# A two-layer graph network in fp32: other order of VectorE's work, statistics shared with ScalarE, other order of loads in the head

## The chip, the cores and the metric

The kernel runs on one core of one Trainium2 chip. The metric is the device time in microseconds of one execution, as the median of three runs. The profiled execution is one more run, with its own time and span.

## The reference

64 samples of 256 tokens with 512 channels go through two layers. Each begins with a layer norm and a relu and ends with a residual sum.

```python
# layer 0
h = maximum(layernorm(x), 0)
q, k, v = h @ Wq.T, h @ Wk.T, h @ Wv.T            # per sample, 256 x 512
rel = adj.T * (q @ k.T)                           # 256 x 256
rel = rel / norm(rel, axis=2)                     # each row by its length
x = x + rel @ v
# layer 1
h = maximum(layernorm(x), 0)
y = adj @ h
x = x + y @ weight + bias
```

All is fp32; adj holds only 0 and 1.

## The kernel before

The kernel takes two samples at a time, a pair: 512 tokens, in four chunks of 128 rows; 32 pairs in all. Chunk c is sample c // 2, token half c % 2. Wq and Wk are multiplied into one matrix M in the head (`before_pairs`), so that the scores are h M h'. Every large product is done by Strassen's scheme in Winograd's form: seven products of half size, numbered 1 to 7, and sums of operands (`left_factors`, `right_operands`) on VectorE; some are split so once more (`two_levels`: g1 to g4 are the products of the second level). Product n goes into a PSUM bank; `take` moves the result out, by a ScalarE copy the first time and by a VectorE addition the next times, always in the order in which the program has them. Products 1, 6, 7 and 4 go into bank_a one after the other, so each of them waits until VectorE or ScalarE has read the one before.

The order of work on TensorE, VectorE and ScalarE is written out by hand: inside `tc.manual_schedule` each of the three carries out its instructions in the order of the program. A list of steps is given to `run_steps`, and a dictionary `side` tells which other work is issued behind which step ("slot" in what follows). DMAs are issued by SP, by ScalarE and by GpSimd.

Software pipelining runs over the pairs: `first_pairs`, then 28 times `steady(i)`, then `last_pairs`. A call of `steady(i)` does, in this order:

- `attend_and_v(i)` (L676): the scores of pair i times v, added to x (take L672), mixed with the rest of v of pair i+1 (L516, L537). When it is done, x of pair i is the input of layer 1. Its token half 0 is complete behind slot 4, its token half 1 behind slot 6.
- `ln1(i)` (L691): statistics of layer 1 by `norm` (L322): for each chunk a BN_STATS (L333) and a BN_AGGR (L334) on VectorE; then the root (L337, L338), its inverse (L341, L342), and the relu on ScalarE (L345), split into an upper and a lower part (L710, L714).
- `scores(i+1)` (L545): seven products (L314), takes L560 (ScalarE) and L562 (VectorE), masks by adj, squares, scaling by the inverse length; then `place`, 16 DMAs on SP that move 32x32 blocks, and `turns` (L592), four VectorE transposes inside those blocks. Together they transpose the scores.
- `g_and_v(i+2)`: h M and h Wv'.
- `gather_steps(i)` (L729): y = adj h (L742), four PSUM tiles, each copied to yt by ScalarE (L746); and `y_steps`, the four sums over yt for the product that follows: `y_steps[0]` (L176), `y_steps[1]` (L177, the operand of product 5; it adds the two channel halves of one token half), `y_steps[2]` (L178, the operand of product 6) and `y_steps[3]` (L179).
- `mix_and_v(i)` (L927): y times `weight` (L302), added to x (take L776), with the second level (L528, L537), whose eight sums over 128x128 blocks `second_of_y` gives (L758); then GpSimd's DMA of the pair.

`norm_by_scalar` (L351) is another form of the statistics, for layer 0: the totals by a ScalarE Copy with an accumulator (L361), the squares by a Square with an accumulator (L367).

The head loads adj, Wq, Wk and the first pair, computes M by one Winograd product (`early=True`: products 1, 2, 5, 6, 3, 7, 4), transposes Wv and looks into adj: `look` (L842) takes the lowest 12 bits of all its elements, and a flag `low_any` tells whether any is set. Every engine reads the flag (L906) and branches to one of two programs, `pairs(True)` or `pairs(False)`.

```python
    y_products, y_steps = gather_steps(i, exact)
    run_steps(y_products, {0: v_steps[1:2], 2: y_steps[0:1], 3: turns})
    y_second = second_of_y(i)
    ...
    run(y_steps[1:2])
    mixed = mix_and_v(i, g, v, {
        0: y_steps[2:4] + totals[0:2], 1: y_second[0:4] + totals[2:4],
```

Of the kernel before, what the change touches and what calls it, by code (L numbers as in the profile page):

```python
# [19 lines left out]
def kernel(  # L20
# [39 lines left out]
    P = 128  # L60
# [21 lines left out]
    X, H, HL, G, V, R, H2, Y, HL2, Y2, second_h = ({} for _ in range(11))  # L82
# [5 lines left out]
    def load(i, queue=nc.sync):  # L88
        X[i] = ring[i % len(ring)]
        queue.dma_start(out=X[i], in_=xs[i])  # L90
# [7 lines left out]
    bias_bc = const.tile([P, D], F32, name="bias_bc")  # L98
    nc.scalar.dma_start(out=adj_sb, in_=adj.rearrange("(c p) n -> p c n", p=P))
    for e in range(DC):  # L100
        nc.sync.dma_start(out=wq_sb[:, e], in_=wq[e * P : (e + 1) * P, :])
        nc.scalar.dma_start(out=wk_sb[:, e], in_=wk[e * P : (e + 1) * P, :])
    load(0)
    ones = const.tile([P, 1], F32, name="ones")
# [5 lines left out]

    def load_wv():
        nc.scalar.dma_start(out=wv_sb, in_=wv.rearrange("(c p) d -> p c d", p=P))
# [209 lines left out]
    def norm(src):  # L322

        st = small.tile([P, TC, 6], F32, tag="st", name="st")
        mv = small.tile([P, TC, 2], F32, tag="mv", name="mv")
        rs = small.tile([P, TC], F32, tag="rs", name="rs")
        nb = small.tile([P, TC], F32, tag="nb", name="nb")  # L330

        def chunk(c):
            nc.vector.bn_stats(st[:, c, :], src[:, c, :])  # L333
            nc.vector.bn_aggr(mv[:, c, :], st[:, c, :])  # L334

        def root():
            nc.vector.tensor_scalar(rs, mv[:, :, 1], 0.0, EPS, op0=ALU.max, op1=ALU.add)  # L337
            nc.scalar.activation(rs, rs, AF.Sqrt)  # L338

        def end():  # L340
            nc.vector.reciprocal(rs, rs)  # L341
            nc.vector.scalar_tensor_tensor(nb, mv[:, :, 0], -1.0, rs, op0=ALU.mult, op1=ALU.mult)  # L342

        def relu(dst, c):
            nc.scalar.activation(  # L345
                dst, src[:, c, :], AF.Relu, bias=nb[:, c : c + 1], scale=rs[:, c : c + 1]
            )

        return [(lambda c=c: chunk(c)) for c in range(TC)], root, end, relu
# [40 lines left out]
    def ln0(i):  # L390

        if i == 0:
            H[i] = blocks.rearrange("p c d e -> p c (d e)")
        else:
            H[i] = work.tile([P, TC, D], F32, tag="hy", name=f"h_{i}")
        h = H[i]
        chunks, root, end, relu = norm(flat(X[i]))
        return chunks, root, end, [(lambda c=c: relu(h[:, c, :], c)) for c in range(TC)]
# [292 lines left out]
    def ln1(i, exact):  # L691
# [3 lines left out]
        chunks, root, end, relu = norm(xt)  # L695
# [62 lines left out]
    def second_of_y(i, pool_tag="h2"):  # L758

        room = work.tile([P, 2, 3, P], F32, tag=pool_tag, name=f"ys2_{i}")  # L760
        factors, steps = {}, []
        for k in (2, 3):
            factors[k], more = left_factors(
                lambda b, d, f=Y[i][k]: f[:, d, ts(b, P)], [room[:, k - 2, n] for n in range(3)]
            )
            steps.append(more)
        Y2[i] = factors
        return steps[0][:2] + steps[1][:2] + steps[0][2:] + steps[1][2:]
# [54 lines left out]
    def before_pairs():  # L823
# [18 lines left out]
        def look():  # L842
            nc.vector.tensor_single_scalar(
                low, adj_sb.rearrange("p c n -> p (c n)").bitcast(I32), 0xFFF, op=ALU.bitwise_and
            )
            nc.vector.tensor_reduce(low_max, low, axis=mybir.AxisListType.X, op=ALU.max)
            pf = ps_m.tile([P, 512], F32, tag="pm", name="pf")
            nc.tensor.matmul(pf[0:1, 0:1], low_max, ones, start=True, stop=True)
            nc.vector.tensor_copy(low_any, pf[0:1, 0:1])
# [20 lines left out]
        def take(t, k, bank, first):  # L870
# [7 lines left out]
        look()  # L878
        transpose_adj()
        run([right_steps[1], left_steps[1]])  # L880
        winograd(product_weights_moving(m_left, m_factors), take, {
            0: [load_wv, left_steps[2], right_steps[2]],
            1: [left_steps[3], left_steps[0]],
            2: [right_steps[0]] + stats[0:1] + [lambda: load(1, nc.scalar)],
            3: stats[1:4] + [root, lambda: load(2, nc.scalar)],
            4: [end] + relus + [right_steps[3]],
            5: m_steps[0:3] + [transpose_wv],
# [49 lines left out]
    def first_pairs(exact):  # L937
# [50 lines left out]
        if exact:  # L988
            nc.vector.tensor_copy(adjt_r, adjt_sb)
        g, v = g_and_v(2, by_slot(layer_1(parts), {  # L990
            1: h_second + [inverse], 2: turned3[0:4], 3: scales + [place],
# [12 lines left out]
            2: y_second[4:8] + [mean] + row_squares[0:2], 3: v_steps[1:2] + row_squares[2:4],  # L1004
            4: turns + rel_steps[0:2] + norm0[0:2], 5: rel_steps[2:4] + v_steps[2:3],
# [3 lines left out]
    def steady(i, exact, relu0, v_last, mixed, v):  # L1009
# [6 lines left out]
        stats, root, end, relus, uppers, lowers = ln1(i, exact)  # L1016
        halves = [stats[b * NC + t] for t in range(NC) for b in range(NB)]
        attend_and_v(i, mixed, v, {
            0: relus0[0:2] + v_last, 1: relus0[2:4] + gs[0:1], 2: gs[1:2],
            3: gs[2:3], 4: gs[3:4] + halves[0:1], 5: halves[1:2],  # L1020
        })
        place_blocks(i + 3)
        if i + 4 < NP:
# [4 lines left out]
            0: halves[2:3], 1: halves[3:4] + h_second[0:1], 2: [root] + h_second[1:4],  # L1028
# [13 lines left out]
        run_steps(y_products, {0: v_steps[1:2], 2: y_steps[0:1], 3: turns})  # L1042
# [5 lines left out]
        run(y_steps[1:2])  # L1048
# [8 lines left out]
    def last_pairs(exact, relu0, v_last, mixed, v):  # L1057
# [62 lines left out]
            0: y_second[0:4] + [root], 1: y_second[4:8] + [end] + relus[0:2] + uppers[0:2],  # L1120
# [10 lines left out]
        ], {0: y_steps[2:4], 1: y_second})  # L1131
# [36 lines left out]
```

## Time and profile before

| | |
|---|---|
| median of three runs | 1705.73 us (1705.2 to 1706.16) |
| profiled execution | 1703.48 us, span 1701.4 us |
| granted TensorE clock | 0.999 |
| TensorE matmul, share of the span | 99% |
| VectorE | 87% |
| ScalarE | 48% |
| GpSimd | 13% |
| one steady pair | 51.7 us |
| bytes moved by DMA | 122.56 MB, 72 GB/s |

The clock is full throughout. A matmul's bar in the profile is longer than the distance to the next one, because matmuls overlap, so the share of 99% does not tell what is lost between them; the starts do. In the timeline a row can stand for several instructions of one form (x4): it then gives the start of the first and the time until the end of the last. PEld is the loading of a matmul's stationary operand, and an instruction name with q (PEq, SPq) is the engine's sequencer.

### The profile page before, as it was taken

How to read it: one execution, taken by the hardware profiler on the slowest of the kernel's cores; microseconds unless marked ns; L12 is line 12 of the kernel's file. 1: busy time of each engine (PE TensorE's matmuls, PEld its weight loads, DVE VectorE, ACT ScalarE, POOL GpSimd, SP SyncE). 2: the span in 40 equal slices, each digit the busy share in tenths (PEclk: the TensorE clock that was granted, in tenths of full speed). 3: DMA queues.
4: the chain of work that ended last, by engine and by line, in shares of the span. 5: the costliest groups of instructions: out<-in, count | busy, mean ns of one | idle time of the engine just before them, and what ended most of it. 6: DMA issues, size and time to landing. Idle time of an engine off the chain costs nothing.

```text
span 1701.4 us, 28459 instructions
## 1 busy us (share of the span) xinstructions
PE 1684.2 (99%) x10274; PEld 1530.6 (90%) x10274; DVE 1472.9 (87%) x3312; ACT 811.3 (48%) x1835; POOL 226.7 (13%) x191
## 2 busy tenths in 40 slices
PE   9999999999999999999999999999999999999997
PEld 7979999999899999999999999999999999999986
DVE  7788889888898888898888988888988889888677
ACT  4455444545445554445544455454455544453331
POOL 1211100111101111001111001110011110011111
PEclk9999999999999999999999999999999999999999
DMA  7414332234332233332343322443323433223101
GB/s 247 63 26 87 84 78 57 55 77 87 79 62 68 53 87 85 77 60 63 65 87 80 83 50 50 87 87 77 60 67 60 87 83 80 55 47 62 38 25 53
DMA packets 425734, 122.56 MB, mean 72 GB/s; under 512 B 398064, under 2 KB 398832, under 8 KB 425584
## 3 DMA queue, kind: packets, MB, share of 16 engines
q1 hardware_dynamic: 412992, 80.28, 25.6%
q0 software_dynamic: 8432, 32.51, 5.2%
q10 hardware_dynamic: 4160, 7.87, 1.3%
q8 instruction: 83, 1.36, 0.3%
q14 instruction: 67, 0.55, 0.1%
HBM read 38.27 MB, written 33.55 MB: 42 GB/s over the span
## 4 chain that ended last, share of the span: by engine, by line
PE 91%; DVE 4%; SPq 2%; DMA 1%; ACT 1%; issue 1%; DVEq 0%; ACTq 0%
PE bank_a L302 24%; PE bank_a L290 12%; PE bank_a L314 7%; PE bank_c L302 6%; PE bank_e L528 6%; PE bank_a L665 6%; PE py L742 6%; PE bank_d L528 5%; PE bank_c L314 3%; PE bank_c L290 3%; PE bank_c L665 3%; PE bank_e L481 3%; SPq L589 2%; PE bank_d L481 2%; PE bank_b L314 2%; PE bank_b L665 1%
## 5 line engine op out<-in xcount | busy, mean ns | idle before, releaser
L726 POOL TENSOR_TENSOR x_ring<-x_ring,bias_bc 128x512 f32<-128x512 f32 x128 | 187.2, 1483 | 667.3 <-DVE rel L562 406.2
L302 PE MATMUL bank_a<-wv_t,ht 128*128 128x256 f32 x768 | 181.7, 379 | 0.0
L290 PE MATMUL bank_a<-ht,m_t 128*128 128x256 f32 x768 | 181.4, 379 | 0.0
L290 PEld LDWEIGHTS bank_a<-ht,m_t 128*128 128x128 f32 x768 | 145.9, 190 | 19.8
L302 PEld LDWEIGHTS bank_a<-wv_t,ht 128*128 128x128 f32 x768 | 143.5, 190 | 18.3
L714 DVE TENSOR_TENSOR h<-h2c,h 128x512 fp32r<-128x512 f32 x128 | 85.4, 689 | 80.0 <-ACT h L710 80.0
L516 ACT COPY v<-bank_a 128x512 f32<-128x512 f32 x96 | 55.1, 574 | 206.5 <-PE bank_a L302 206.5
L367 ACT ACTIVATE blocks<-x_ring,sm 128x512 f32<-128x512 f32 x112 | 80.8, 722 | 125.3 <-DVE sm L364 123.5
L742 PE MATMUL py<-adjt_r,h 128*128 128x256 f32 x1024 | 127.1, 281 | 0.5 <-DVE h L714 0.4
L345 ACT ACTIVATE h2c<-x_ring,nb,rs 128x512 f32<-128x512 f32 x128 | 97.3, 809 | 58.0 <-DVE nb L342 51.9
L302 PE MATMUL bank_a<-w_t,ys 128*128 128x256 f32 x512 | 121.4, 380 | 2.2 <-DVE x_ring L776 2.2
L742 PEld LDWEIGHTS py<-adjt_r,h 128*128 128x128 f32 x1024 | 120.9, 189 | 1.0 <-DVE h L714 0.9
L797 POOL DMA_DIRECT2D out_dram<-x_ring x31 | 24.0, 773 | 723.3 <-issue 522.9
L380 ACT ACTIVATE h<-x_ring,nb,rs 128x512 f32<-128x512 f32 x112 | 82.0, 802 | 66.0 <-PE bank_e L528 66.0
L302 PEld LDWEIGHTS bank_a<-w_t,ys 128*128 128x128 f32 x512 | 96.7, 190 | 16.4 <-DVE x_ring L776 3.0
L746 ACT COPY yt<-py 128x512 f32<-128x512 f32 x128 | 74.9, 588 | 70.4 <-PE py L742 47.3
L776 DVE TENSOR_TENSOR x_ring<-bank_a,x_ring 128x512 f32<-128x512 f32 x128 | 87.9, 687 | 23.2 <-PE bank_a L302 23.2
L314 PE MATMUL bank_a<-ht,gt 128*128 128x128 f32 x744 | 101.2, 279 | 0.0
L333 DVE BATCH_NORM_STATS2 st<-x_ring 128x6 f32<-128x512 f32 x144 | 97.6, 678 | 0.4
L560 ACT COPY rel<-bank_a 128x256 f32<-128x256 f32 x96 | 35.7, 372 | 129.6 <-PE bank_a L314 111.1
L314 PEld LDWEIGHTS bank_a<-ht,gt 128*128 128x128 f32 x744 | 90.4, 192 | 2.8
L453 DVE STREAM_TRANSPOSE ht<-blocks 128x256 f32<-128x256 f32 x248 | 87.7, 407 | 0.7 <-DMA blocks<-h 0.7
(223 smaller groups left out, 4012.5 us busy)
## 6 DMA issues: line engine op xcount, KB each, us to landing
blocks<-h SPq DMA_DIRECT2D x496, 64.0 KB, 2.3
out_dram<-x_ring POOLq DMA_DIRECT2D x31, 1024.0 KB, 4.8
x_ring<-in_x_dram SPq DMA_DIRECT2D x28, 1024.0 KB, 5.6
placed<-rel SPq DMA_DIRECT2D x496, 32.0 KB, 2.0
x_ring<-in_x_dram ACTq DMA_DIRECT2D x4, 1024.0 KB, 5.3
wq_sb<-in_L_gnn_Wq_dram SPq DMA_DIRECT2D x4, 256.0 KB, 4.8
wk_sb<-in_L_gnn_Wk_dram ACTq DMA_DIRECT2D x4, 256.0 KB, 6.0
wv_sb<-in_L_gnn_Wv_dram ACTq DMA_DIRECT2D x1, 1024.0 KB, 5.6
```

Source lines behind the costliest of these rows:

```text
L290: nc.tensor.matmul(bank[:, e * HT_ : (e + 1) * HT_], right[n][:, d, ts(e, P)], left[n][:, d, :], start=(start and e == 0 and d == 0), stop ...
L302: nc.tensor.matmul(bank[:, b * HD : (b + 1) * HD], left[n][:, d, ts(b, P)], right[n][:, d, :], start=(start and b == 0 and d == 0), stop=( ...
L314: nc.tensor.matmul(bank[:, ts(b, P)], right[n][:, d, ts(b, P)], left[n][:, d, ts(b, P)], start=(start and b == 0 and d == 0), stop=(d == H ...
L333: nc.vector.bn_stats(st[:, c, :], src[:, c, :])
L345: nc.scalar.activation(dst, src[:, c, :], AF.Relu, bias=nb[:, c : c + 1], scale=rs[:, c : c + 1])
L453: nc.vector.transpose(ht[:, d, half].rearrange("p (b n) -> p b n", b=NB), by_half[:, :, half, d])
L528: nc.tensor.matmul(out, left[k][n], right[k][n], start=start, stop=True, skip_group_check=True)
L665: nc.tensor.matmul(bank[:, ts(b, HD)], left[n][:, b], right[n][:, b], start=(start and b == 0), stop=True, skip_group_check=True,)
L714: nc.vector.tensor_sub(dst[:, 1, c, :], whole_h[c], dst[:, 0, c, :].bitcast(F32))
L726: (lambda c=c: add(xt[:, c, :], xt[:, c, :], bias_bc, ALU.add)) for c in range(TC)
L742: nc.tensor.matmul(pm[:, d, :], left[:, b * NC + m, ts(d0 + d, P)], right, start=(n == 0), stop=(n == len(terms) - 1),)
L776: nc.vector.tensor_add(xt[block], bank.rearrange("p (b e) -> p b e", b=NB), xt[block])
```

## The change

Five things are changed.

- In `steady`, `turns` leave slot 3 of the gather and go behind `y_steps[1]`, so that VectorE does the sum first and then the four transposes.
- `norm` can be given a scratch tile, `junk`. Then chunks 0 and 2 (token half 0 of both samples) get their mean and their squares by ScalarE (`totals`, `squares`), with two small VectorE operations: the sign change of the means and the division of the squares (`variances`). Chunks 1 and 3 stay with BN_STATS. It is used for layer 0 of the first pair (with room in h) and for layer 1 in `steady` (with room behind the tile of `second_of_y`, which gets 10 blocks instead of 6). In `steady` the totals are issued behind slot 4 of `attend_and_v`, the squares behind slot 5, the variances and chunk 1 behind slot 0 of the scores, chunk 3 behind slot 1.
- Head: Wq and Wk are loaded by four blocks of 256 rows x 256 columns instead of four blocks of 128 rows; adj is loaded after them; Wv's load is issued at once instead of behind product 1. The look at adj and its transposes move from the start to slots 4 and 5 of the product; reading the flag's sum from PSUM becomes `find`.
- `first_pairs`: the scaling of the scores and `place` go one slot earlier, ahead of four block transposes.
- `last_pairs`: the eight sums of the second level are split over slots 1 and 2, four each, in the last two products.

```diff
+    for k in range(2):
+        for j in range(2):
+            block = (slice(None), slice(j * HC, (j + 1) * HC), slice(k * HD, (k + 1) * HD))
+            nc.sync.dma_start(out=wq_sb[block], in_=wq.rearrange("(c p) d -> p c d", p=P)[block])
+            nc.scalar.dma_start(out=wk_sb[block], in_=wk.rearrange("(c p) d -> p c d", p=P)[block])
     nc.scalar.dma_start(out=adj_sb, in_=adj.rearrange("(c p) n -> p c n", p=P))
-    for e in range(DC):
-        nc.sync.dma_start(out=wq_sb[:, e], in_=wq[e * P : (e + 1) * P, :])
-        nc.scalar.dma_start(out=wk_sb[:, e], in_=wk[e * P : (e + 1) * P, :])
     load(0)
+    nc.scalar.dma_start(out=wv_sb, in_=wv.rearrange("(c p) d -> p c d", p=P))
...
-    def norm(src):
+    def norm(src, junk=None):
...
+        def totals():
+            for c in (0, 2):
+                nc.scalar.activation(
+                    junk, src[:, c, :], AF.Copy, scale=1.0 / D, accum_out=mv[:, c, 0:1]
+                )
+
+        def squares():
+            minus = small.tile([P, TC], F32, tag="minus", name="minus")
+            nc.vector.tensor_single_scalar(minus[:, 0::2], mv[:, 0::2, 0], -1.0, op=ALU.mult)
+            for c in (0, 2):
+                nc.scalar.activation(
+                    junk, src[:, c, :], AF.Square, bias=minus[:, c : c + 1],
+                    accum_out=mv[:, c, 1:2],
+                )
+
+        def variances():
+            nc.vector.tensor_scalar(
+                mv[:, 0::2, 1], mv[:, 0::2, 1], 0.0, 1.0 / D, op0=ALU.max, op1=ALU.mult
+            )
...
+        chunks = [(lambda c=c: chunk(c)) for c in range(TC)]
+        if junk is not None:
+            chunks = [totals, squares, variances] + chunks[1::2]
...
-        room = work.tile([P, 2, 3, P], F32, tag=pool_tag, name=f"ys2_{i}")
+        rooms = 6 if pool_tag == "hs2" else 10
+        room = work.tile([P, rooms * P], F32, tag=pool_tag, name=f"ys2_{i}")
+        junk[i] = room[:, 6 * P :]
...
-        look()
-        transpose_adj()
         run([right_steps[1], left_steps[1]])
         winograd(product_weights_moving(m_left, m_factors), take, {
-            0: [load_wv, left_steps[2], right_steps[2]],
+            0: [left_steps[2], right_steps[2]],
             1: [left_steps[3], left_steps[0]],
             2: [right_steps[0]] + stats[0:1] + [lambda: load(1, nc.scalar)],
-            3: stats[1:4] + [root, lambda: load(2, nc.scalar)],
-            4: [end] + relus + [right_steps[3]],
-            5: m_steps[0:3] + [transpose_wv],
+            3: stats[3:4] + stats[1:2] + [right_steps[3], lambda: load(2, nc.scalar)],
+            4: stats[4:5] + [look, stats[2], root, end] + relus,
+            5: m_steps[0:3] + [transpose_wv, find, transpose_adj],
             6: m_steps[3:4],
         }, early=True)
...
-            1: h_second + [inverse], 2: turned3[0:4], 3: scales + [place],
+            1: h_second + [inverse], 2: scales + [place] + turned3[0:4],
...
-        halves = [stats[b * NC + t] for t in range(NC) for b in range(NB)]
         attend_and_v(i, mixed, v, {
             0: relus0[0:2] + v_last, 1: relus0[2:4] + gs[0:1], 2: gs[1:2],
-            3: gs[2:3], 4: gs[3:4] + halves[0:1], 5: halves[1:2],
+            3: gs[2:3], 4: stats[0:1] + gs[3:4], 5: stats[1:2],
         })
...
-            0: halves[2:3], 1: halves[3:4] + h_second[0:1], 2: [root] + h_second[1:4],
+            0: stats[2:4], 1: stats[4:5] + h_second[0:1], 2: [root] + h_second[1:4],
...
-        run_steps(y_products, {0: v_steps[1:2], 2: y_steps[0:1], 3: turns})
+        run_steps(y_products, {0: v_steps[1:2], 2: y_steps[0:1]})
...
-        run(y_steps[1:2])
+        run(y_steps[1:2] + turns)
...
-            0: y_second[0:4] + [root], 1: y_second[4:8] + [end] + relus[0:2] + uppers[0:2],
+            0: [root], 1: y_second[0:4] + [end] + relus[0:2] + uppers[0:2], 2: y_second[4:8],
...
-        ], {0: y_steps[2:4], 1: y_second})
+        ], {0: y_steps[2:4], 1: y_second[0:4], 2: y_second[4:8]})
```

## The prediction

> **What bounds the kernel now.** I read the page first: the busy shares, then the chain that ended last.
>
> ```profile
> PE 1684.2 (99%) x10274; PEld 1530.6 (90%) x10274; DVE 1472.9 (87%) x3312; ACT 811.3 (48%) x1835; POOL 226.7 (13%) x191
> ...
> PE 91%; DVE 4%; SPq 2%; DMA 1%; ACT 1%; issue 1%; DVEq 0%; ACTq 0%
> ```
>
> TensorE holds the chain almost throughout, and no edit takes a matmul away, so only its stalls can move. They are found in the timeline as distances between the starts of neighbouring matmuls above 0.216 us (256 columns) or 0.112 (128). That makes some 34.5 us: 6 in the first 30 us, 18.4 in the 28 steady pairs of 51.7 us each, 7.6 after 1580 us. Two places of a steady pair matter.
>
> Place A, the product of y with the last weight, in pair 4: VectorE's timeline, then TensorE's (start, duration, engine, line, operation, idle before).
>
> ```profile
> 319.77 0.68 DVE L176 TENSOR_TENSOR ys<-yt 128x512 f32<-128x512 f32 x1
> 320.42 1.42 DVE L592 STREAM_TRANSPOSE turned<-placed 128x256 f32<-128x256 f32 x4
> 321.77 0.65 DVE L177 TENSOR_TENSOR yt<-yt 128x512 f32<-128x512 f32 x1
> 322.69 0.69 DVE L776 TENSOR_TENSOR x_ring<-bank_a,x_ring 128x512 f32<-128x512 f32 x1 [0.27 <-PE bank_a L302]
> 323.30 0.68 DVE L178 TENSOR_TENSOR ys<-yt 128x512 f32<-128x512 f32 x1
> ```
> ```profile
> 320.69 1.89 PE L302 MATMUL bank_a<-w_sb,yt 128*128 128x256 f32 x8
> 322.57 1.97 PE L302 MATMUL bank_c<-w_sb,yt 128*128 128x256 f32 x8
> 324.37 1.89 PE L302 MATMUL bank_a<-w_t,ys 128*128 128x256 f32 x8
> ```
>
> The four transposes fill the time until ScalarE's fourth copy of y ends (321.47). Then comes the sum (L177), for which product five (322.57) waits; then L776, which empties bank_a, and L178, which product six (324.37) needs. Six loses nothing. Over 28 pairs five loses 6.5 us, 0.23 a pair; in six of them the transposes' DMA lands late and it is 0.5 to 0.8.
>
> Place B, the scores, VectorE and then product four:
>
> ```profile
> 345.47 0.69 DVE L672 TENSOR_TENSOR x_ring<-bank_a,x_ring 128x512 f32<-128x512 f32 x1 [0.37 <-PE bank_a L665]
> 346.08 0.41 DVE L537 TENSOR_TENSOR v<-bank_e,v 128x256 f32<-128x256 f32 x1
> 346.41 0.68 DVE L537 TENSOR_TENSOR v<-bank_d,v 128x512 f32<-128x512 f32 x1
> 347.01 0.68 DVE L333 BATCH_NORM_STATS2 st<-x_ring 128x6 f32<-128x512 f32 x1
> 347.72 0.18 DVE L334 BATCH_NORM_AGGREGATE mv<-st 128x2 f32<-128x6 f32 x1
> 347.82 0.66 DVE L672 TENSOR_TENSOR x_ring<-bank_a,x_ring 128x512 f32<-128x512 f32 x1
> 348.40 0.41 DVE L537 TENSOR_TENSOR v<-bank_e,v 128x256 f32<-128x256 f32 x1
> 348.73 0.68 DVE L333 BATCH_NORM_STATS2 st<-x_ring 128x6 f32<-128x512 f32 x1
> ```
> ```profile
> 353.06 1.16 PE L314 MATMUL bank_a<-ht,gt 128*128 128x128 f32 x8
> ```
>
> VectorE is idle before 345.47, so it is caught up there; from 347.01 it runs without a gap to L562 (352.59), which empties bank_a for product four. That product already loses 0.17 us a pair.
>
> In the head, TensorE's timeline and what is said of the flag that picks the program's branch:
>
> ```profile
> 20.64 1.89 PE L302 MATMUL bank_a<-wk_t,wq_sb 128*128 128x256 f32 x8
> 22.36 1.91 PE L431 MATMUL pt<-ident,blocks 128*128 128x128 f32 x16
> ```
> ```profile
> L849 DVE CAST low_any<-pf x1: 145/145/145, 6.1 to 6.1; 1x1 int32<-1x1 f32 x1
> ...
> L906 PEldq TENSOR_LOAD <-low_any x1: 486/486/486, 20.3 to 20.3; - x1
> ```
>
> The flag is ready at 6.2 us, so TensorE's sequencer can read it at 20.3, ahead of the matmuls, and the branch costs nothing.
>
> **What the Trainium skill says.** Perfetto Trace Analysis, "Sequencer Loop": an instruction goes into its engine's queue and waits there for its semaphores, while a control instruction is executed by the sequencer. The trace agrees: in place A L776 starts only after what stands before it, and the flag's load runs 2 us ahead. DMA: Bandwidth & Descriptors, "Issuing engines are not separate DMA queues": transfers from SP and ACT share the same 16 engines and interleave. Here the 16 engines are full from 4 to 12 us (384 and 370 GB/s). VectorE: DVE Perf Modes, "Two Vector instructions with no wait between them": an accumulating operation is two instructions. On ScalarE the trace shows the pair, 0.63 and 0.19 us (L361).
>
> **The change, part by part.** The sum is against the profiled execution (1703.48 us, span 1701.4); the median of the runs is 2.25 higher.
>
> *Sum ahead of the transposes (28 steady pairs).* No work is added. The sum cannot use the 0.7 us that the transposes filled, since it adds both channel halves and needs the fourth copy: it starts at 321.50 instead of 321.77. Behind it, in VectorE's order: sum 0.60 (start to start), transposes 1.34, L776 0.61, L178 0.68: ready at 324.73, TensorE at 324.78. Product six without any loss would be at 320.69 + 16 x 0.216 = 324.15. So it loses 0.63 plus about 0.08 for the first interval: 0.70. The copy's end moves by under 0.1 between pairs, so this holds in each. Product five's wait goes, late DMAs are covered (the transposes start 1.7 later), but six waits for the queue instead. Three hundredths more for the second-level sums behind it: 0.73 - 0.23 = +0.50, x 28 = **+14.0**. Bounds +11 to +17.
>
> *Statistics (28 pairs).* Off VectorE: two chunks, 0.68 + 0.18 each; on: two small operations of 0.17. ScalarE gets two Copy (0.81 start to start) and two Square (0.85). In place B: ScalarE's copy of v (L516) starts at 344.61, the totals run 345.10 to 346.63. VectorE's sign change follows L537 at 347.01, the squares run 347.20 to 348.87. VectorE now does L672 when TensorE is done with it (347.4, not 347.82) and L537 at 348.0, is free at 348.33, and then stands before the variances until 348.90. The next chunk starts at 348.98 instead of 348.73, and behind it stands everything up to L562. Product four is 0.25 later: **+7.0**. ScalarE's L560 comes 0.07 late, which its bank's next product covers by 0.2. The chain through ScalarE has no example in the trace: if it is hidden, product four's own 0.17 goes (-4.8); if L560 and one more wake-up count too, +0.45 (+12.6). I take +0.25, since every duration in it has a row.
>
> *Head.* Wq and Wk land as before, in 1 KB pieces; product one needs one block of each and not two. Product five needs the fourth Wq block (8.4 landed now, 8.6 then), the sum (0.69): 9.5 instead of 11.98, -2.5. But Wv's load no longer waits behind ScalarE's first copy (issue 9.57); it is issued while the engines are full and shares them with x. Some 0.75 MB more lie ahead of x's end: 12.05 becomes about 14.3 at 377 GB/s. The totals of x stand on ScalarE before product six's copy: 14.3 + 1.6 + 0.6 = 16.5, and product seven, which reuses that bank, starts there instead of 17.16. The flag's matmul and four transposes of the adjacency move from idle time into the stream: 0.55. Product four is then at about 20.6, as before: the gain is spent. Now the flag: on VectorE, from 16.5, come an addition 0.6, a chunk 0.8, the look 1.2, the statistics' end 1.1, an addition 0.7, three m steps 2.15, two copies 1.2, the cast 0.15: 24.4. Reading it and branching took TensorE 0.75 at 20.3; L431 comes at 25.2 and not 22.36: +2.8. Of that 0.7 returns, since product five of the next stage no longer waits (26.46). **+2.1**, bounds -2 (x lands as before, the flag hidden) to +3.5.
>
> *First pairs.* The scales and 16 score DMAs go ahead of four transposes, 1.6 earlier; the turns that need them (123.3) waited for no DMA, so nothing is won. ScalarE's copy of v stands behind the scales: **+0.2** (0 to +0.6).
>
> *Tail.* In the last product but one L776 of product six stood behind eight 128x128 steps (it ran at 1670.01); with four of them it runs at 1669.1: -0.95. In the last one likewise, 1688.46 to 1687.41: -1.05. **-2.0** (-1.5 to -3).
>
> Sum: 14.0 + 7.0 + 2.1 + 0.2 - 2.0 = **+21.3**: 1724.8 for the profiled execution, 1727.0 for the median.
>
> **Rivals.**
> 1. *VectorE's relief carries through* (faster). VectorE is 87% busy and loses about 1.3 us a pair; if it reaches both places ahead of time, the waits go: -6.5 - 4.8, with head, first pairs and tail -11.0: 1694.7. It decides only if the sum can start by 320.8 and the squares end by 348.3. Against it: VectorE was idle or waiting just before both places, so being ahead buys nothing there.
> 2. *ScalarE's chain is hidden.* Place A as worked out, B at 0 to -4.8: about 1717.
> 3. *Place B is worse*, the +0.45 a pair: 1732.6.
> 4. *Place A is smaller*, product six hidden for a reason not seen and B as worked out: 1713.
>
> **Numbers.** Chances: mine 0.53, rival 1 0.11, 2 0.14, 3 0.13, 4 0.09. The predicted time is the likeliest case's, 1727. The range, 1714 to 1737, takes in rivals 2 and 3, the bounds of A and the head, and leaves out rival 1. A measurement of this kernel tells about 0.2% from no change (1702.3 to 1709.1): faster 0.11, the same 0.03 (the edges of 1 and 4), slower 0.86.
>
> **What would show it.** Right: the transposes of the scores start after the sum, and product six in bank_a begins 0.6 to 0.8 us late in every steady pair, while five starts on time; L562 of product seven ends 0.25 later after TensorE's L665; the pair takes 52.5 us instead of 51.73; the flag's load on TensorE begins at about 24. Wrong: a steady pair of 51.5 us or less, or product six on time. Then the time is 1700 or below, and my order of VectorE's queue or its start at the fourth copy is at fault.

## The result, and the profile after

The kernel is slower: 1727.42 us (median of four runs, 1727.29 to 1727.8) beside 1705.95 for the kernel before (four runs, 1705.2 to 1707.43); ratio 1.0125, 95% interval 1.0108 to 1.0143. The profiled execution took 1727.55 us, span 1725.5. The lines of the new kernel are shifted against those shown so far: L333 is now L335, L592 is L617, L672 is L697, L776 is L804, L562 is L587, L537 is L562 and L431 is L456.

The page of the new kernel, busy shares and then the chain:

```profile
PE 1691.6 (98%) x10274; PEld 1531.6 (89%) x10274; DVE 1430.1 (83%) x3254; ACT 895.4 (52%) x2067; POOL 218.5 (13%) x191
...
PE 66%; DVE 15%; SPq 7%; ACT 5%; issue 3%; DMA 3%; DVEq 0%; ACTq 0%
```

VectorE lost 43 us of work and ScalarE gained 84, yet VectorE's share of the chain went from 4% to 15%: it has less to do and is waited for more. Where this happens is read from the starts of TensorE's matmuls. The execution is cut at the first matmul of a gather:

| stretch (profiled executions, us) | before | after | difference | predicted |
|---|---|---|---|---|
| start to the first gather | 107.24 | 110.95 | +3.71 | head +2.1 |
| to the first steady gather | 54.06 | 54.91 | +0.85 | first pairs +0.2 |
| 28 steady pairs | 1451.27 | 1471.18 | +19.91 | +21.0 |
| to the gather of the last pair but one | 39.70 | 39.72 | +0.02 | 0 |
| to the gather of the last pair | 24.29 | 24.89 | +0.60 | -0.95 |
| to the end of the span | 24.84 | 23.84 | -1.00 | -1.05 |

**Place A.** VectorE's timeline of the new kernel, then TensorE's; columns as before (start, duration, engine, line, operation, idle before and who ended it):

```profile
326.49 0.69 DVE L176 TENSOR_TENSOR ys<-yt 128x512 f32<-128x512 f32 x1
328.34 0.69 DVE L177 TENSOR_TENSOR yt<-yt 128x512 f32<-128x512 f32 x1 [1.17 <-ACT yt L771]
328.95 1.42 DVE L617 STREAM_TRANSPOSE turned<-placed 128x256 f32<-128x256 f32 x4
330.29 0.65 DVE L804 TENSOR_TENSOR x_ring<-bank_a,x_ring 128x512 f32<-128x512 f32 x1
330.86 0.67 DVE L178 TENSOR_TENSOR ys<-yt 128x512 f32<-128x512 f32 x1
```
```profile
327.52 1.89 PE L302 MATMUL bank_a<-w_sb,yt 128*128 128x256 f32 x8
329.25 1.89 PE L302 MATMUL bank_c<-w_sb,yt 128*128 128x256 f32 x8
331.59 1.99 PE L302 MATMUL bank_a<-w_t,ys 128*128 128x256 f32 x8 [0.45 <-DVE ys L178]
```

VectorE now idles 1.17 us before the sum, where the transposes used to be, and does them when product six (331.59) is next in line. Product five starts 1.73 after product one, that is on time; product six 2.34 after five. Over the 28 pairs six loses 0.725 us a pair (0.62 before it and 0.105 behind its first matmul), five nothing (0.233 before). With place B, below, a steady pair takes 52.54 us on the mean, 51.83 before.

**Place B.** VectorE, then product four of the scores on TensorE:

```profile
354.33 0.16 DVE L346 TENSOR_SCALAR minus<-mv 128x2 f32<-128x2 f32 x1
354.71 0.69 DVE L697 TENSOR_TENSOR x_ring<-bank_a,x_ring 128x512 f32<-128x512 f32 x1 [0.22 <-PE bank_a L690]
355.32 0.41 DVE L562 TENSOR_TENSOR v<-bank_e,v 128x256 f32<-128x256 f32 x1
356.22 0.17 DVE L354 TENSOR_SCALAR mv<-mv 128x2 f32<-128x2 f32 x1 [0.49 <-ACT ys L348]
356.30 0.69 DVE L335 BATCH_NORM_STATS2 st<-x_ring 128x6 f32<-128x512 f32 x1
```
```profile
360.63 1.16 PE L314 MATMUL bank_a<-ht,gt 128*128 128x128 f32 x8 [0.15 <-DVE rel L587]
```

VectorE, freed of two chunks here (0.68 and 0.18 us each), stands 0.49 us before the variances (L354) until ScalarE's second square (L348) is done. Product four loses 0.414 us a pair instead of 0.172.

**Head.** TensorE's timeline of the new kernel:

```profile
20.57 2.00 PE L302 MATMUL bank_a<-wk_t,wq_sb 128*128 128x256 f32 x8
24.83 3.46 PE L456 MATMUL pt<-ident,blocks 128*128 128x128 f32 x16 [2.27 <-ACT adjt_sb L888]
28.08 2.08 PE L290 MATMUL bank_a<-ht,m_sb 128*128 128x256 f32 x8
```

The transposes of h (L456) start 2.47 us later than before (22.36), because TensorE stands at the branch until the flag has been read, at 24.0:

```profile
L934 PEldq TENSOR_LOAD <-low_any x1: 488/488/488, 24.0 to 24.0; - x1
```

In addition the sixteen transposes take 3.46 us and not 1.91: one in 0.2 us instead of 0.109. What that is, the last section shows.

### The profile page after: what moved, and what is told of

Read it like the earlier page. It is cut to its first block, busy times and chain, and to the rows that moved or that the text cites. A ratio compares the mean times of both kernels' runs of the same rounds, so it can differ in the third digit from the quotient of the medians.

```text
span 1725.5 us, 28632 instructions
## 1 busy us (share of the span) xinstructions
PE 1691.6 (98%) x10274; PEld 1531.6 (89%) x10274; DVE 1430.1 (83%) x3254; ACT 895.4 (52%) x2067; POOL 218.5 (13%) x191
## 3 DMA queue, kind: packets, MB, share of 16 engines
q1 hardware_dynamic: 413504, 80.28, 25.2%
q8 instruction: 83, 1.36, 0.3%
## 4 chain that ended last, share of the span: by engine, by line
PE 66%; DVE 15%; SPq 7%; ACT 5%; issue 3%; DMA 3%; DVEq 0%; ACTq 0%
PE bank_a L302 19%; PE bank_a L290 12%; SPq L468 7%; PE py L767 7%; PE bank_e L553 4%; PE bank_c L302 4%; PE bank_c L290 3%; PE bank_e L506 3%; PE bank_d L553 3%; PE bank_a L690 3%; ACT h L405 3%; PE bank_a L314 3%; DVE st L335 2%; PE bank_d L506 2%; DVE turned L617 2%
## 5 line engine op out<-in xcount | busy, mean ns | idle before, releaser
L751 POOL TENSOR_TENSOR x_ring<-x_ring,bias_bc 128x512 f32<-128x512 f32 x128 | 180.5, 1430 | 681.6 <-ACT h2c L367 651.5
L739 DVE TENSOR_TENSOR h<-h2c,h 128x512 fp32r<-128x512 f32 x128 | 85.5, 691 | 80.8 <-ACT h L735 80.8
L367 ACT ACTIVATE h2c<-x_ring,nb,rs 128x512 f32<-128x512 f32 x128 | 97.3, 809 | 59.8 <-DVE nb L364 50.1
L697 DVE TENSOR_TENSOR x_ring<-bank_a,x_ring 128x512 f32<-128x512 f32 x116 | 79.7, 687 | 39.5 <-PE bank_a L690 39.5
L804 DVE TENSOR_TENSOR x_ring<-bank_a,x_ring 128x512 f32<-128x512 f32 x128 | 86.9, 679 | 8.4 <-PE bank_a L302 4.4
L492 ACT COPY g<-bank_a 128x512 f32<-128x512 f32 x96 | 56.0, 583 | 56.3 <-PE bank_a L290 56.3
```

Source lines behind the costliest of these rows:

```text
L367: nc.scalar.activation(dst, src[:, c, :], AF.Relu, bias=nb[:, c : c + 1], scale=rs[:, c : c + 1])
L751: (lambda c=c: add(xt[:, c, :], xt[:, c, :], bias_bc, ALU.add)) for c in range(TC)
L804: nc.vector.tensor_add(xt[block], bank.rearrange("p (b e) -> p b e", b=NB), xt[block])
```

## The experiments

Each is an edit of the changed kernel, unless said otherwise. The runs of the kernel before that stood beside them had medians of 1705.39 to 1706.45. Losses per pair are means over the 28 steady pairs of one profiled execution, taken from the starts of the matmuls.

**1. The transposes back ahead of the sum.**

```diff
-        run_steps(y_products, {0: v_steps[1:2], 2: y_steps[0:1]})
+        run_steps(y_products, {0: v_steps[1:2], 2: y_steps[0:1], 3: turns})
...
-        run(y_steps[1:2] + turns)
+        run(y_steps[1:2])
```

> The changed kernel with the four block transposes back in slot 3 of the gather, ahead of the sum; all else as changed. Queue theory (the transposes' 1.34 us now stand between the sum and the sum for product six): product six loses under 0.1 us a pair instead of 0.73, product five gets back its 0.23; 0.49 x 28 = 13.8 us less, 1713.6. Rival (the late operand comes from ScalarE's statistics and not from the order on VectorE): product six stays late, 1726 to 1728. Rival (both together): about 1720.

Measured: 1715.53 us (1713.68 to 1716.75), ratio to before 1.0054 (1.0037 to 1.0071). Product six loses nothing that can be seen; product five loses 0.35 and not 0.23, since in seven of the pairs the transposes' DMA was so late that five waited 0.6 to 1.1 us. The queue's order is the cause of place A: of its price of 13.8 us, 10.6 came back in the 28 pairs of the profiled execution (11.9 between the medians). The later DMAs, 0.12 us a pair more than before the change, are the rest.

**2. Layer 1's statistics back on VectorE.**

```diff
-        stats, root, end, relus, uppers, lowers = ln1(i, exact, junk.pop(i - 1))
+        stats, root, end, relus, uppers, lowers = ln1(i, exact)
+        halves = [stats[b * NC + t] for t in range(NC) for b in range(NB)]
...
-            3: gs[2:3], 4: stats[0:1] + gs[3:4], 5: stats[1:2],
+            3: gs[2:3], 4: gs[3:4] + halves[0:1], 5: halves[1:2],
...
-            0: stats[2:4], 1: stats[4:5] + h_second[0:1], 2: [root] + h_second[1:4],
+            0: halves[2:3], 1: halves[3:4] + h_second[0:1], 2: [root] + h_second[1:4],
```

> The changed kernel with layer 1's statistics of the steady pairs on VectorE alone, as before the change. Theory (VectorE stands before the variances until ScalarE's squares end): product four of the scores loses 0.17 us a pair instead of 0.41; 0.24 x 28 = 6.7 us less, 1720.7. Rival (that loss comes from somewhere else in the change): no difference, 1726.5 to 1728. Rival (VectorE's relief is worth something elsewhere in the pair): slower than 1728.

Measured: 1721.33 us (1720.68 to 1721.45), ratio 1.0092 (1.0075 to 1.0109). Product four loses 0.173 a pair again, and product six of place A still its 0.73, so that wait does not come from the statistics. The shared statistics cost 6 us; the work that they take off VectorE is worth nothing in this order.

**3. The variances behind chunk 3.** The same work, in another place.

```diff
-            0: stats[2:4], 1: stats[4:5] + h_second[0:1], 2: [root] + h_second[1:4],
+            0: stats[3:4], 1: stats[4:5] + [stats[2]] + h_second[0:1], 2: [root] + h_second[1:4],
```

> The changed kernel with the variances issued behind chunk 3 instead of ahead of chunk 1; no work added or taken away. Theory (the stand before the variances is the whole cost of place B): VectorE reaches the addition that empties bank_a in time, product four loses under 0.1 us a pair instead of 0.41; 9 to 11.5 us less, 1716 to 1718.5. Rival (ScalarE's own chain is late, its four more operations delay its copies of the scores): product four stays at 0.3 to 0.4, 1726 to 1728.

Measured: 1724.33 us (1723.77 to 1726.22), ratio 1.0111 (1.0094 to 1.0128): neither of the two. Product four's loss is gone (0.007 a pair), as the theory said. But product seven of h M, which reuses bank_a, now waits for ScalarE's copy of product six (L492) and loses 0.35. Following that back along the timelines: ScalarE's copy stands behind its scales and squares, the squares need the masked scores, and the two mask multiplications on VectorE (L590) took 1.6 us each, where the changed kernel's first one took 0.68. VectorE's timeline of this run, then GpSimd's:

```profile
359.92 3.23 DVE L590 TENSOR_TENSOR rel<-rel,adjt_sb 128x512 f32<-128x512 f32 x2
```
```profile
359.66 2.94 POOL L751 TENSOR_TENSOR x_ring<-x_ring,bias_bc 128x512 f32<-128x512 f32 x2 [14.74 <-ACT h2c L367]
```

The earlier relus (ScalarE's L367) free GpSimd's addition of the bias (L751) 0.26 us ahead of the first mask; in the trace the additions end at 360.92 and 362.60, and each mask ends 0.56 us after one of them, as if it had only then had its turn. The Trainium skill, SBUF — State Buffer, "Who interferes with whom", has this: a VectorE instruction with two inputs in SBUF contends with a GpSimd instruction that reads SBUF, and whoever comes first holds the shared port to its end. Three more runs try it.

**4. The same, with the additions in another order.**

```diff
+        bias = add_bias(i)
...
-            4: lowers[2:3] + sums[0:1] + add_bias(i),
+            4: lowers[2:3] + sums[0:1] + bias[2:4] + bias[0:2],
```

> The kernel with the variances behind chunk 3, and GpSimd's four additions of the bias in the steady pairs in the order of chunks 2, 3, 0, 1, so that they start some 9 us later, after the masks. Theory (in the run before, the additions, started earlier by the earlier relus, held VectorE's mask multiplications, 1.6 us each instead of 0.68, and through the squares ScalarE's copy for the product of h M): the masks take 0.68, that product doesn't wait, place B loses under 0.1 us a pair; 0.4 x 28 = 11 us less than the changed kernel, 1716. Rival 1 (ScalarE's relus are in the way themselves): as the run before, 1724. Rival 2 (the additions now hold VectorE's subtractions and sums in the products of h M and h Wv): 0.2 to 0.6 us a pair come back there, 1722 to 1733.

Measured: 1726.39 us (1726.24 to 1727.44), ratio 1.0118 (1.0101 to 1.0135). This tells nothing of the theories: GpSimd is not among the engines whose order is written by hand, its first addition started at 359.76 as in the run before (359.66), and product seven lost the same 0.35. It is a repetition of experiment 3, on another chip, and lies 2 us above it. In the 28 pairs of the two profiled executions the difference is 1.7 us, and 1.6 of that is in the gathers, whose matmuls ran 1.5% slower; why was not followed.

**5. The additions left out.** The kernel of experiment 3 without the bias in the 28 steady pairs; that part of the sum isn't computed.

```diff
-            4: lowers[2:3] + sums[0:1] + add_bias(i),
+            4: lowers[2:3] + sums[0:1],
```

> The kernel with the variances behind chunk 3, without GpSimd's additions of the bias in the 28 steady pairs (that part of the sum is left out); nothing else is moved, so relus and inverse stay as early as in that kernel. Theory (the additions hold VectorE's masks): both masks take 0.68 us, the product of h M waits under 0.05 us a pair instead of 0.35; 1714 to 1716. Rival (the early relus on ScalarE were in the way, and moving them back was the cure): the product of h M still waits 0.3 or more, 1723 to 1726.

Measured: 1714.92 us (1714.4 to 1716.35), ratio 1.0054 (1.0037 to 1.0071). VectorE's timeline:

```profile
357.25 0.68 DVE L590 TENSOR_TENSOR rel<-rel,adjt_sb 128x512 f32<-128x512 f32 x1
358.20 0.69 DVE L590 TENSOR_TENSOR rel<-rel,adjt_sb 128x512 f32<-128x512 f32 x1 [0.27 <-ACT rel L585]
```

Without an addition beside them both masks take 0.68 and 0.69, and neither product waits any more. GpSimd's additions were the cause, not the early relus.

**6. The additions kept, the relus later.** The kernel of experiment 3, with the root's inverse and the relus one slot later.

```diff
-            3: [end] + relus[0:1], 4: relus[1:2],
+            4: [end] + relus[0:2],
```

> The kernel with the variances behind chunk 3, and the inverse of the root (two small operations) and both relus one slot later in the scores, behind the addition that empties bank_a; no work added. Theory (GpSimd's additions, freed by the relus, hold the masks): the first addition starts at least 0.6 us later against the scores, the first mask takes 0.68 and is done before it, the second waits at most once; the product of h M waits under 0.1 us and the scores' product four under 0.1; place B 0.4 us a pair less than in the changed kernel, 11 us, 1716. Rival (ScalarE itself is too full there, and the later relus push its copies): the product of h M waits 0.35 or more, 1724 to 1728.

Measured: 1714.55 us (1714.09 to 1715.73), ratio 1.0051 (1.0034 to 1.0068). VectorE's timeline, then GpSimd's:

```profile
358.85 0.68 DVE L590 TENSOR_TENSOR rel<-rel,adjt_sb 128x512 f32<-128x512 f32 x1
360.16 1.06 DVE L590 TENSOR_TENSOR rel<-rel,adjt_sb 128x512 f32<-128x512 f32 x1 [0.63 <-ACT rel L585]
```
```profile
359.26 3.10 POOL L751 TENSOR_TENSOR x_ring<-x_ring,bias_bc 128x512 f32<-128x512 f32 x2 [15.40 <-ACT h2c L367]
```

The first addition now begins 0.41 us after the first mask's start and not 0.26 before it; that mask takes 0.68, the second 1.06. Products four and seven lose under 0.01 a pair. The 28 pairs take 1460.54 us, beside 1460.48 in the run without additions: this order costs nothing more than leaving the additions out.

**7. The transposes still later**, in the product of y.

```diff
-        run(y_steps[1:2] + turns)
+        run(y_steps[1:2])
...
-            3: rel_steps[0:2] + row_squares[2:4], 4: root0 + rel_steps[2:4] + end0,
+            3: turns + rel_steps[0:2] + row_squares[2:4], 4: root0 + rel_steps[2:4] + end0,
```

> The changed kernel with the transposes moved further back, to slot 3 of the mix ahead of the sums over them, so that neither the sum for product five nor that for product six has them ahead of it. Queue theory: neither product waits, 0.73 x 28 = 20.3 us less, 1707. Rival (the transposes only carry the wait to the next place, the addition that empties bank_a for product four of the mix or the first product of the scores times v): 0.3 to 0.6 us a pair come back there, 1715 to 1724.

Measured: 1732.68 us (1730.69 to 1734.6), ratio 1.0161 (1.0144 to 1.0178): the rival's mechanism, and worse than it said. VectorE, then TensorE:

```profile
334.43 1.41 DVE L617 STREAM_TRANSPOSE turned<-placed 128x256 f32<-128x256 f32 x4
335.87 0.42 DVE L176 TENSOR_TENSOR rel<-turned 128x256 f32<-128x256 f32 x1
336.33 0.42 DVE L177 TENSOR_TENSOR turned<-turned 128x256 f32<-128x256 f32 x1
336.68 0.68 DVE L804 TENSOR_TENSOR x_ring<-bank_a,x_ring 128x512 f32<-128x512 f32 x1
```
```profile
337.41 1.99 PE L302 MATMUL bank_a<-w_t,yt 128*128 128x256 f32 x8 [0.65 <-DVE x_ring L804]
```

Five and six wait for nothing, but product four of this stage waits until L804, behind the transposes, has emptied bank_a: 0.92 us a pair where six lost 0.73. From the first L804 (327.73) to that one VectorE runs without a gap, so of the 1.34 us of the transposes 0.92 come out as a wait for the next bank.

**8. Two transposes ahead of the sum, two behind.**

```diff
-        run_steps(y_products, {0: v_steps[1:2], 2: y_steps[0:1]})
+        run_steps(y_products, {0: v_steps[1:2], 2: y_steps[0:1], 3: turns[0:2]})
...
-        run(y_steps[1:2] + turns)
+        run(y_steps[1:2] + turns[2:4])
```

> The changed kernel with two of the four transposes in slot 3 of the gather ahead of the sum, and two behind it. Queue theory: two (0.67 us) fit into VectorE's idle time before the fourth copy of y, the other two mostly into its idle time before product one ends (0.49), so product five starts on time but for late DMAs and product six loses under 0.1; 0.6 to 0.7 us a pair less than the changed kernel, 1708 to 1711. Rival (any transposes behind the sum cost product six their whole time): product six loses 0.3 to 0.4, 1717 to 1719.

Measured: 1709.4 us (19 runs, 1707.93 to 1711.24), ratio 1.0016 (1.0009 to 1.0023). VectorE:

```profile
325.28 0.76 DVE L617 STREAM_TRANSPOSE turned<-placed 128x256 f32<-128x256 f32 x2
326.41 0.69 DVE L177 TENSOR_TENSOR yt<-yt 128x512 f32<-128x512 f32 x1 [0.37 <-ACT yt L771]
327.02 0.76 DVE L617 STREAM_TRANSPOSE turned<-placed 128x256 f32<-128x256 f32 x2
327.71 0.65 DVE L804 TENSOR_TENSOR x_ring<-bank_a,x_ring 128x512 f32<-128x512 f32 x1
```

VectorE has two holes (idle times) here, one before ScalarE's fourth copy of y (1.17 us in the changed kernel) and one before product one is done (0.49 us where no transposes stand there, as in experiment 7). Two transposes fit into the first and most of two into the second; place A loses 0.10 us a pair. That is less than before the change (0.23), since with only two of them ahead of the sum product five is late in two of the pairs alone (0.5 and 0.2 us); with all four ahead it was late by 0.1 us or more in 19.

**9. Head and first pairs.** The cast of the flag goes ahead of the m steps; in the first pairs the scales and `place` go back.

```diff
-            5: m_steps[0:3] + [transpose_wv, find, transpose_adj],
+            5: [transpose_wv, find] + m_steps[0:3] + [copy_wv, transpose_adj],
...
-            1: h_second + [inverse], 2: scales + [place] + turned3[0:4],
+            1: h_second + [inverse], 2: turned3[0:4], 3: scales + [place],
```

(`copy_wv` is the second half of `transpose_wv`, its four copies out of PSUM.)

> The changed kernel with two edits in stages that don't touch. Head: the flag's cast goes ahead of the three m steps and of the copies of Wv's transposes on VectorE. First pairs: scales and place back behind the four transposes of slot 2. Theory for the head (the flag, waited for at the branch, holds the transposes of h back): the cast comes at about 20.7, TensorE waits under 1 us, the transposes of h start at about 23.0 (when ScalarE's relus end) instead of 24.8 and run at 0.11 us each, the first product of h M starts at 26.1 instead of 28.1. Rival (ScalarE's copies, not the flag, are the limit): first product at 27.5 or later. Theory for the first pairs: the wait of product five of the mix at 116 us goes from 0.84 to 0.25. Together 2.3 us less, 1725.1; rival 1727.

Measured: 1725.5 us (1724.78 to 1726.12), ratio 1.0112 (1.0095 to 1.0129). The cast ran at 20.23, the transposes of h began at 22.20 behind product four without a wait, and the first product of h M at 25.20. The first gather came at 108.44, and product five of the first product of y waited 0.25 us instead of 0.84. So the flag, late by VectorE's queue, was the wait in the head, and the move of scales and `place` the one in the first pairs. The gain in the head is smaller than the 2.5 us between the two first gathers: the changed kernel's profiled execution had also lost some 1.7 us to a lower clock (last section). Against the executions of its head at full clock, with first gathers at 108.96 to 109.29, it is 0.5 to 0.8, because products one and five of h M now wait 0.9 and 0.6 us for ScalarE's copy and VectorE's sum.

**10. No addition beside the last product but one.** The bias of the last pair is left out.

```diff
-            4: lowers[0:2] + relus[2:4], 5: uppers[2:4] + add_bias(c), 7: lowers[2:4],
+            4: lowers[0:2] + relus[2:4], 5: uppers[2:4], 7: lowers[2:4],
```

> The changed kernel without the bias of the last pair: the four additions by GpSimd that run beside the last product but one are left out. Theory (GpSimd's additions hold VectorE's two 128x128 steps, 1.36 and 1.24 us instead of 0.28): both steps take 0.28, the second-level product g2 doesn't wait, the last but one product is 1.5 us shorter; 1725.9. Rival (the two steps wait for something else): steps stay at 1.2 to 1.4, 1727.4.

Measured: 1725.13 us (1723.91 to 1726.59), ratio 1.0112 (1.0095 to 1.0128). The changed kernel's VectorE and GpSimd in that product, then VectorE in this run:

```profile
1693.52 0.69 DVE L804 TENSOR_TENSOR x_ring<-bank_a,x_ring 128x512 f32<-128x512 f32 x1
1694.13 0.28 DVE L178 TENSOR_TENSOR ys<-yt 128x128 f32<-128x128 f32 x1
1694.44 0.29 DVE L179 TENSOR_TENSOR ys<-yt,ys 128x128 f32<-128x128 f32 x1
1694.65 1.36 DVE L178 TENSOR_TENSOR ys<-ys 128x128 f32<-128x128 f32 x1
1696.05 1.24 DVE L179 TENSOR_TENSOR ys<-ys,ys 128x128 f32<-128x128 f32 x1
1697.21 0.41 DVE L562 TENSOR_TENSOR x_ring<-bank_e,x_ring 128x256 f32<-128x256 f32 x1
```
```profile
1694.46 2.68 POOL L751 TENSOR_TENSOR x_ring<-x_ring,bias_bc 128x512 f32<-128x512 f32 x2 [14.68 <-DVE ys L178]
```
```profile
1693.19 0.28 DVE L178 TENSOR_TENSOR ys<-ys 128x128 f32<-128x128 f32 x1
1693.51 0.29 DVE L179 TENSOR_TENSOR ys<-ys,ys 128x128 f32<-128x128 f32 x1
1693.72 0.41 DVE L562 TENSOR_TENSOR x_ring<-bank_e,x_ring 128x256 f32<-128x256 f32 x1
```

Two steps of 0.28 us took 1.36 and 1.24 beside the additions, and L562 behind them, which empties bank_e, let TensorE wait 1.58 us. Without the additions the stretch takes 23.34 us instead of 24.89, and that is 0.95 less than before the change (24.29): the split's own gain. The last stretch is 0.63 us shorter as well (23.21 instead of 23.84): two subtractions of VectorE with both inputs in SBUF (L739), on which the last gather waits, take 1.28 us there and 1.81 beside the additions. That wait the kernel before has too.

**11 and 12. What remains, put on the kernel before.** First the split of experiment 8 and the split of the eight sums in the very last product only; then, in addition, the shared statistics in the order of experiment 6. Head, first pairs and last product but one stay as before the change.

```diff
-        run_steps(y_products, {0: v_steps[1:2], 2: y_steps[0:1], 3: turns})
+        run_steps(y_products, {0: v_steps[1:2], 2: y_steps[0:1], 3: turns[0:2]})
...
-        run(y_steps[1:2])
+        run(y_steps[1:2] + turns[2:4])
...
-        ], {0: y_steps[2:4], 1: y_second})
+        ], {0: y_steps[2:4], 1: y_second[0:4], 2: y_second[4:8]})
```

> The kernel before the change with two of the four transposes behind the sum, and with the eight sums of the second level split in the very last product only. Theory: place A loses 0.10 us a pair as in the run with the transposes split, and not 0.23, 3.8 us; the last product is 1.0 shorter; 1701.1. Rival (the gain of the split came from the changed kernel's other orders): 1704.5 to 1706.

> As the run just named, and with the shared statistics in the steady pairs, variances behind chunk 3, inverse and relus one slot later; head, first pairs and last but one product as before the change. Theory: place B loses under 0.02 us a pair instead of 0.17, another 4.5 us; 1696.5. Rival (as in the run with the variances last, the wait moves to the product of h M, 0.35 us a pair): 1706.

Measured: 1699.77 us (1698.4 to 1700.56), ratio 0.9964 (0.9949 to 0.9978); and 1694.73 us (1694.37 to 1695.89), ratio 0.9935 (0.9918 to 0.9951). Place A loses 0.11 and 0.10 us a pair, place B 0.17 and under 0.01. The page of the second one:

```profile
PE 1679.8 (99%) x10274; PEld 1527.6 (90%) x10274; DVE 1434.1 (85%) x3256; ACT 886.9 (52%) x2059; POOL 217.8 (13%) x191
...
PE 94%; DVE 3%; DMA 1%; SPq 1%; issue 0%; ACT 0%; ACTq 0%; DVEq 0%
```

VectorE and ScalarE have within 1% the busy time of the changed kernel, which is 33 us slower. The idea of sharing the statistics was good for 5 us (1699.77 to 1694.73); the order made it a loss.

## Why the prediction was right, and where its terms were not

**Place A, +14.0: right.** The predicted loss of product six was 0.70 and 0.03 for the second-level sums; 0.725 was measured, five's 0.23 went, and the difference is +0.49 a pair, 13.8 us. The sum did start only with the fourth copy. (The late DMAs before the change hit five pairs by 0.5 to 0.8 us, not six as the prediction has it; the mean stands.) Experiment 1 confirms the cause, experiments 7 and 8 the reading of the holes.

**Place B, +7.0: right.** +0.24 a pair was measured, with the stand before the variances where it was foreseen (0.49 us until 356.22; 0.57 was worked out). Experiment 2 gives back 6 us. Experiment 3 shows that the stand was the whole cost at product four, and experiments 5 and 6 that the relief of rival 1 exists once nothing stands in the way: 10.6 us in the 28 pairs between the changed kernel and experiment 6, 12.9 between the medians.

**Head, +2.1: right, once the clock is set apart.** x landed at 14.24 (14.3 foreseen, though 0.75 MB at 377 GB/s, added to 12.05, make 14.0 to 14.1), product seven started at 16.27 (16.5), product four at 20.57 (20.6), the cast at 23.81 (24.4), the transposes at 24.83 (25.2). Product five came at 10.30 and not at 9.5, since the fourth block of Wq landed at 9.46; the 0.8 was taken up by product seven's wait. What the working did not have is TensorE's clock, granted at half for 3.41 us behind the wait. In the profiled execution that cost some 1.7 us, half of it, and the stretch to the first gather grew by 3.7. Such a stretch comes in some executions and not in others, with both heads (last section). Those without one put the first gather at 108.96, 109.28 and 109.29 with the new head (experiments 7, 5 and 10) and at 107.24 with the old: +1.72 to +2.05, 1.9 on the mean, though with a single execution for the old head. Of the head's changes only the place of the flag was tried by itself; what the new order of loads does alone was not.

**First pairs, +0.2: too small.** Product five of the first product of y waits 0.59 longer. Place B of the first call of `steady`, which belongs to this stretch, adds 0.24. The prediction bounded this at +0.6 and gave it 0.2, for ScalarE's copy of v alone; what product five waits for is VectorE's sum (L177 at 116.41). The timelines show the way: the four scales (L607, 1.7 us) now stand ahead of ScalarE's casts of h (L735), which start 2.62 us before the gather and not 4.23. VectorE's subtraction that needs the first cast (L739, 108.98) waits 0.80 us for it, where before the change it did not wait, and from there the queue runs without a gap to L177, 5.46 us behind the gather's start instead of 4.87. In experiment 9, with the scales back, it is 4.87 again. The prediction asked after the copy of v behind the scales and not after the casts.

**Tail, -2.0: half wrong.** The very last product gained 1.00 (1.05 foreseen). In the last but one the foreseen gain of 0.95 is there, but 1.55 us were lost to GpSimd's additions, which the prediction's step left out: it moved four operations on VectorE and asked which TensorE product waits, and not which engine runs beside them at their new time. Experiment 10 shows both numbers.

The sum by stages, with the head at 1.9: 1.9 + 0.85 + 19.9 - 0.4 = 22.2; the medians differ by 21.5, the prediction said 21.3. Tail and first pairs came out 1.6 and 0.65 higher than foreseen, steady pairs and head 1.1 and 0.2 lower. Places A and B, nearly all of the time, were foreseen by their cause; that the total came within 0.2 us is luck, since these errors offset each other.

## What to carry to other kernels

Before moving work on an engine with a fixed order, list the holes of that engine (its idle times) and what ends each; a hole that ends with another engine's last result can be filled and not shortened, and what filled it will stand somewhere else. Taking work off an engine gains nothing while it must stand behind the engine that took it over: put the operation that needs the result as late in the queue as its own reader allows. And whatever is moved, look which engine shares a memory port with it at the new time, because an earlier result also frees the neighbour earlier. Where TensorE waits for some 2 us, look at its clock in the short stretch behind the wait before a difference is put down to the wait alone.

## What the hardware showed that was not expected

GpSimd's addition with both inputs in SBUF holds VectorE's operations with two SBUF inputs that begin while it runs, until it ends: 128x128 steps of 0.28 us took 1.36 and 1.24, 128x512 masks of 0.68 took 1.6. An operation that was there first is not held (the first mask of experiment 6). The kernel before pays this too, unnoticed: the second mask of its pairs takes 1.23 us, but no product waits for it. Additions with one input in PSUM went on beside it: L494 took 0.65 and 0.67 us at 370.6 and 371.2 in experiment 4, under GpSimd's additions of 369.2 to 371.7, and the same in experiment 5, which has no additions.

TensorE has two paces in these executions, one half of the other: a matmul of 128 columns comes 0.109 to 0.112 us after the last one or 0.213, one of 256 columns 0.216 or 0.427. A slice in the page's row of the granted clock is 43 us long and hides this; asked for a short stretch, the trace shows the clock. In that view, first the changed kernel behind the branch, then experiment 7 (stretch, its length, busy time and instructions of PE, PEld, DVE, ACT and POOL, then the granted clock, the DMA share and GB/s):

```profile
25.10:28.40 3.30, 3.30 (x17) 3.30 (x16) 1.18 (x2) 1.83 (x4) 2.04 (x4) 0.50 0.02 5
```
```profile
24.70:28.00 3.30, 3.30 (x24) 3.10 (x24) 1.95 (x3) 2.07 (x5) 2.66 (x4) 1.00 0.02 5
```

TensorE's timeline of experiment 7, to be compared with that of the changed kernel above:

```profile
20.42 1.99 PE L302 MATMUL bank_a<-wk_t,wq_sb 128*128 128x256 f32 x8
24.69 1.94 PE L456 MATMUL pt<-ident,blocks 128*128 128x128 f32 x16 [2.27 <-ACT adjt_sb L888]
26.46 1.89 PE L290 MATMUL bank_a<-ht,m_sb 128*128 128x256 f32 x8
```

The wait is the same 2.27 us, the clock is not. The Trainium skill, TensorE: Matmul & The Clock Gate, "Part 1: The HAM clock gate", says that the array runs at half rate until a window of activity, some 3.4 us, which runs on freely, has been busy, and again after an idle one. The clock records of these traces agree in the length: nine of the fourteen profiled executions have half clock in the head, for 3.41 us each (twice that in experiment 12), after 3.41, 6.83 or 20.48 us at full clock, that is one, two or six times 3.41. The first matmuls of every execution, until about 4 us, run at 0.213 us too, so the clock of the kernel before is not full from the very start.

What the traces add is that the window need not be idle as a whole. Cut each trace into pieces of 3.41 us from the first entry of its clock record (between 4.1 and 7.1 us), and count a matmul as busy for its distance at the pace of the moment. Then each of the nine pieces at full clock in which TensorE was idle for 2.17 us or more is followed by half clock; of all others, with up to 2.02 us, none is. This is an estimate from the starts of the matmuls. It says why the same wait at the branch, some 2.4 us between matmuls, cost another 1.7 us in some executions only: in the changed kernel and experiments 1, 2, 3, 4 and 8 at least 2.17 us of it lay in one piece; in experiments 5, 6, 7 and 10 the border of two pieces went through it. Several shorter waits in one piece do the same, as in experiments 11 and 12 with the old head. No run moved such a wait on purpose, so the limit stands on these executions alone.
